# Eight of ten head blocks turned by VectorE and a trip through DRAM instead of by TensorE, in one Perceiver layer

## The chip, the core and the metric

One core of a Trainium2 chip runs the whole layer as one program. The metric is the device time of that program in microseconds (us), lower is better. Its engines work side by side, each through its own list of instructions in order: TensorE (PE; PEld is its weight load), VectorE (DVE), ScalarE (ACT), GpSimd (POOL) and SyncE (SP), which here does nothing but issue DMA transfers. An instruction waits on semaphores that other engines or landed transfers raise; while it waits, everything behind it on its engine waits too.

## The reference, cut to what matters

A layer of three parts: attention of 256 latent rows over 4096 context rows and over themselves, a Mamba block, and a mixture of 32 experts. All is 32-bit float. The change lies in the attention part:

```python
q = (x @ wq).reshape(B, L, 16, 128); k = (x @ wk).reshape(B, L, 4, 128); v = x @ wv
q = rms_norm(q, q_norm_w);  k = rms_norm(k, k_norm_w)
k_ctx = rms_norm((h_ctx_kv @ wk_ctx).reshape(B, T, 4, 128), k_norm_w);  v_ctx = h_ctx_kv @ wv_ctx
q = q * cos + rotate_half(q) * sin;  k = k * cos + rotate_half(k) * sin
scores = einsum('blhd,bmhd->bhlm', q, concat(k_ctx, k)) / sqrt(128) + mask
out = softmax(scores) @ concat(v_ctx, v);  return out @ wo
```

The scores contract over the 128 numbers of a head, so queries and keys must stand with that dimension on the partitions, while a projection leaves them with the rows on the partitions. Each block of 128 rows by 4 heads by 128 numbers must therefore be turned.

## The kernel before, in words

**Projections (5 to 84 us in the profile).** The 256 latent rows are two tiles (`t` = 0, 1). `self_block` makes one head block: four matmul steps (each is two passes in the profile) project it into `ps_self` (L211), `norm_rope` (L429 to L442) applies norm and rotation, and the returned `turn` (L464 to L469) turns it with four PE transposes into PSUM (`selfT`) and one ACT copy into `kT0` or `qT`. There are ten such blocks: two of keys (`wk`), then eight of queries (`wq[0]` to `wq[3]`, two each). Between them stand the first context tile's keys and values (`ps_k`, `ps_v`, with PE transposes `kTp`) and the latents' values (`ps_v0`). `norm_rope` goes through ACT (copy `raw`, four squares `sq` with sums `ss` in `head_squares`, L242 to L248), DVE (L437 to L440, the scale `pv` at L188) and POOL (power `r` at L189, product L441).

**Attention (from 84 us).** Stage `s` = 0 takes the latents' own keys, `s` = 1 to 8 a context tile of 512 keys each. A step is one score (`scT`, L542), its exponential on ACT (`prT`, L545), on the diagonal a mask on DVE (L548), the row sums on DVE (`lacc`, L551 or L553) and the product with the values (`oT`, L562); at the end of a pair of head group and tile DVE takes `oT` out (L566 or L568). The code keeps two steps between a score and its product. In stages 1 to 7 the keys and values of the next context tile are made beside it by a fast product (`fast_steps`): seven pieces (`p1`, `p6`, `p2`, `p7`, `p5`, `p4`, `p3`) for each half, spread evenly over the 32 steps. At the end of `p4` and `p3` a key block is normed (`key_rms`) and turned by `key_blocks` (L281 to L288): DVE transposes 32 by 32 squares, four transfers write them to DRAM tile `kd`, a fifth reads them back into `kT` as a turned block. Those transfers, the next context tile (`load_ctx`) and zeros for the experts' buffers (`clear`, L497 to L506) all go through SP's one list.

**What sets the order.** A scheduler orders every engine's list by its own estimate of when things will be ready, within the dependencies; `tc.issue_after(i)` lets what follows stand no earlier than instruction `i`, and `tc.keep_in_program_order` fixes a transfer's place among the others so marked. Tiles come from pools whose buffers are reused: `ps_tp` has one PSUM buffer (tag `tp`), `ps_mm` two, `krp` two per tag (`kraw`, `sq`), `wpool` six (`w`: `wk`, `wq[0]`, `wv`, `wq[1..3]`, then `wo[0..2]`, `fast0..2`, in that order of the code).

The fast product needs weight sums (`fast_weights`, L323 to L330: three ACT copies, and at L330 a difference on POOL that overwrites part of `wkv`) and sums of the context tile (`sums` in `fast_steps`, L342 to L345, four POOL operations per tile).

Of the kernel before, what the change touches and what calls it, by code (L numbers as in the profile page):

```python
# [11 lines left out]
FP = mybir.dt.float32  # L12
# [3 lines left out]
ALU = mybir.AluOpType  # L16
# [3 lines left out]
P = 128  # L20
L = 256
NT = L // P
DM = 512
# [4 lines left out]
NH = 16  # L28
NKV = 4
REP = NH // NKV  # L30
HD = 128
# [36 lines left out]
def perceiver_layer(ctx: ExitStack, tc: tile.TileContext, a: dict, out: bass.AP):  # L68
# [53 lines left out]
    kd = [tc.dram_tile((CK // P, NKV, HD, P), FP, name=f"kd{c}") for c in range(NC)]  # L122
    sums_d = [tc.dram_tile((SH, P), FP, name=f"sums{t}") for t in range(NT)]
# [9 lines left out]
    def layer(ctx, bounded):  # L133
# [44 lines left out]
        def wpiece(src, name):  # L178

            n = src.shape[1]  # L180
            w = wpool.tile([P, KD, 512], FP, tag="w", name=name)
            nc.sync.dma_start(w[:, :, :n], src.rearrange("(k p) n -> p k n", p=P))
            return w
# [58 lines left out]
        def head_squares(raw):  # L242

            sq = krp.tile([P, REP, HD], FP, tag="sq", name="sq")
            ss = small.tile([P, REP], FP, tag="ss", name="ss")
            for h in range(REP):
                S.activation(sq[:, h, :], raw[:, h, :], AF.Square, accum_out=ss[:, h:h + 1])  # L247
            return ss  # L248

# [12 lines left out]
        def context_tiles(c):  # L262
# [18 lines left out]
            def key_blocks(i):  # L281

                tr = krp.tile([P, NKV * HD], FP, tag="sq", name="tr")
                V.transpose(tr, raws.pop(i).rearrange("p h d -> p (h d)"))
                for b in range(0, P, 32):
                    nc.sync.dma_start(kd[c][i, :, :, b:b + 32].rearrange("h (j a) k -> a h j k", a=32),
                                      tr[b:b + 32, :].rearrange("a (h j k) -> a h j k", h=NKV, k=32))
                nc.sync.dma_start(kT[:, :, i * P:(i + 1) * P], kd[c][i].rearrange("h d k -> d h k"))  # L288
# [34 lines left out]
        def fast_weights(sums):  # L323
# [6 lines left out]
            G.tensor_tensor(b12, b22, b12, ALU.subtract)  # L330

        def fast_steps(c):
# [77 lines left out]
            sums()  # L410
# [17 lines left out]

        def norm_rope(ps, t, tb):  # L429
# [11 lines left out]
            G.tensor_tensor(o, o, r.unsqueeze(2).to_broadcast([P, REP, HD]), ALU.mult)  # L441
            return o  # L442

        kT0 = kvp.tile([P, NKV, CK], FP, tag="kT", name="kT0")
# [14 lines left out]
        def self_block(t, w, tb, dst):  # L459
            ps = ps_mm.tile([P, 512], FP, tag="mm", name="ps_self")  # L460
            project(ps, lambda k: xT[:, k, t * P:(t + 1) * P], lambda k: w[:, k, :])
            o = norm_rope(ps.rearrange("p (h d) -> p h d", d=HD), t, tb)

# [32 lines left out]

        def clear(n):  # L497

            per = -(-ROUNDS * NE // (NC - 1))
            e0, e1 = n * per, min((n + 1) * per, ROUNDS * NE)  # L500
            nc.sync.dma_start(xg[e0 * P:e1 * P, :].rearrange("(e p) d -> p e d", p=P),
                              xn[:, 0:1, :].to_broadcast([P, e1 - e0, DM]))
            if n == 0:
                for y in (ye, ye2):
                    nc.sync.dma_start(y[(NE - TAIL) * P:, :].rearrange("(e p) d -> p e d", p=P),
                                      xn[:, 0:1, :].to_broadcast([P, TAIL + 1, DM]))  # L506

        nc.sync.dma_start(by_channel, a["by_channel"])
        nc.sync.dma_start(by_head, a["by_head"].partition_broadcast(P))


        wo = [wpiece(a["wo"][j * 512:(j + 1) * 512, :], f"wo{j}") for j in range(3)]
        fast_weights(sums)
        w_x = []
# [11 lines left out]
        def bounded_attention(beside):  # L526
# [50 lines left out]
            for s in range(NC + 1):  # L577
# [6 lines left out]
                if 0 < s < NC:  # L584
                    if s + 1 < NC:
                        load_ctx(s + 1)
                    clear(s - 1)
                    extra = fast_steps(s)
# [129 lines left out]
        def mamba_memory():  # L718
# [3 lines left out]
            for t in range(NT):  # L722
                m["csT", t] = krp.tile([P, REP, HD], FP, tag="sq", name="csT")[0:SH, 0, :]
# [705 lines left out]
```

## Time and profile before

| what | us |
|---|---|
| median of 3 runs (1017.68 to 1018.71) | 1018.51 |
| the profiled execution: its time | 1019.19 |
| the profiled execution: its span | 1017.4 |
| PE busy in the span | 996.1 |
| first score of attention (`scT`) | 84.06 |
| first `ps_o` matmul (output projection) | 694.46 |

The profile is of one execution. Times in its views count from the start of the span. In a timeline line the numbers are start and duration in us, then engine, source line, operation, out<-in, shape, count, and in brackets how long the engine had been idle and who ended that. In a line of the table by stretches each engine has its busy time and, in brackets, how many instructions; then the granted TensorE clock, the share of the DMA engines, and GB/s. A PE matmul's end is modelled, and matmuls are pipelined: what counts is the distance from one start to the next. All line numbers L are those of the kernel before unless "after" is said.

### The profile page before, as it was taken

What the parts mean: (1) busy time and instruction counts of PE and PEld (TensorE: products, weight loads), DVE (VectorE), ACT (ScalarE), POOL (GpSimd) and SP (SyncE); (2) the same over time, 40 slices, a digit from 0 to 9 for tenths busy, and PEclk for the clock granted to TensorE, in tenths of its full rate; (3) what the DMA queues carried; (4) which work ended last, traced back from release to release, by engine and by line L of the source; (5) the groups of instructions that cost most, each with busy time, mean ns of one, the idle gap of its engine ahead of it and who ended that gap; (6) DMA issues with size and microseconds to landing.
All of it is one profiled execution on the core that took longest, in us unless ns stands there. A gap on an engine that the chain in (4) does not pass through costs nothing.

```text
span 1017.4 us, 9099 instructions
## 1 busy us (share of the span) xinstructions
PE 996.1 (98%) x2818; PEld 480.9 (47%) x2818; DVE 495.4 (49%) x975; ACT 384.6 (38%) x870; POOL 156.9 (15%) x156
## 2 busy tenths in 40 slices
PE   7999999999999999999999999999999999999997
PEld 3444444444444444444444444444656554555553
DVE  4347454445444454544544544575885653322233
ACT  3456444443443443443443434442445431222210
POOL 4343001001001101100200200000131322000022
PEclk9999999999999999999999999999999999999999
DMA  9997021110210301301301202500264358999833
GB/s 335 375 404 303 0 42 50 34 31 30 64 26 16 83 11 32 82 10 32 83 2 40 63 0 42 156 10 0 94 200 148 114 208 318 357 353 371 291 116 95
DMA packets 115435, 127.73 MB, mean 126 GB/s; under 512 B 63377, under 2 KB 78642, under 8 KB 114226
## 3 DMA queue, kind: packets, MB, share of 16 engines
q1 hardware_dynamic: 108272, 111.52, 33.9%
q0 software_dynamic: 2208, 8.39, 2.3%
q10 hardware_dynamic: 4898, 7.16, 1.9%
q8 instruction: 24, 0.39, 0.2%
q14 instruction: 33, 0.27, 0.1%
HBM read 88.76 MB, written 38.29 MB: 125 GB/s over the span
## 4 chain that ended last, share of the span: by engine, by line
PE 91%; DMA 2%; DVE 2%; POOL 2%; issue 1%; ACT 1%; SPq 0%; POOLq 0%; DVEq 0%; ACTq 0%
PE oT L562 23%; PE scT L542 22%; PE ps_kv L350 17%; PE ps_egu L211 7%; PE ps_self L211 3%; PE ps_ye L1256 2%; PE ps_o L754 2%; PE ps_ye L1259 1%; PE ps_v L211 1%; PE ps_k L211 1%; PE ps_xbc L211 1%; PE ps_out L944 1%; PE xgTp L1201 1%; PE total L1247 1%; DMA lm<-sums 1%
## 5 line engine op out<-in xcount | busy, mean ns | idle before, releaser
L553 DVE TENSOR_TENSOR lacc<-lacc,prT 128x512 f32<-128x512 f32 x260 | 182.7, 704 | 246.3 <-ACT prT L545 245.5
L545 ACT ACTIVATE prT<-scT,bq,rk 128x512 f32<-128x512 f32 x256 | 198.3, 775 | 228.0 <-PE scT L542 223.1
L562 PE MATMUL oT<-prT,v 128*128 128x512 f32 x536 | 272.2, 592 | 1.3 <-DVE prT L548 1.3
L542 PE MATMUL scT<-qT,kT 128*128 128x512 f32 x536 | 272.3, 592 | 0.0
L562 PEld LDWEIGHTS oT<-prT,v 128*128 128x128 f32 x536 | 101.7, 190 | 129.4 <-issue 109.3
L542 PEld LDWEIGHTS scT<-qT,kT 128*128 128x128 f32 x536 | 101.2, 190 | 124.6 <-issue 123.1
L189 POOL TENSOR_TENSOR rk<-pv,mhalf 128x4 f32<-128x4 f32 x32 | 32.3, 1011 | 357.8 <-DVE pv L188 357.1
L247 ACT ACTIVATE sq<-kraw 128x128 f32<-128x128 f32 x128 | 38.3, 301 | 94.0 <-DVE kraw L368 93.9
L1216 DVE TENSOR_TENSOR hid<-si,ps_egu 128x128 f32<-128x128 f32 x32 | 9.2, 288 | 94.2 <-ACT si L1214 94.2
L350 PE MATMUL ps_kv<-fast,fast 128*128 128x512 f32 x112 | 52.6, 592 | 0.0
L350 PE MATMUL ps_kv<-wkv,fast 128*128 128x512 f32 x112 | 52.6, 592 | 0.0
L350 PE MATMUL ps_kv<-wkv,ctx 128*128 128x512 f32 x112 | 52.6, 592 | 0.0
L568 DVE TENSOR_TENSOR oacc<-oT,oacc 128x512 f32<-128x512 f32 x64 | 43.7, 683 | 0.0
L1170 POOL DMA_INDIRECT yk<-ye,row_y x12 | 13.3, 1105 | 137.5 <-PE ps_egu L211 134.1
L350 PEld LDWEIGHTS ps_kv<-wkv,ctx 128*128 128x128 f32 x112 | 21.3, 190 | 26.8 <-issue 23.7
L350 PEld LDWEIGHTS ps_kv<-fast,fast 128*128 128x128 f32 x112 | 21.3, 190 | 26.8 <-issue 21.8
L350 PEld LDWEIGHTS ps_kv<-wkv,fast 128*128 128x128 f32 x112 | 21.3, 190 | 26.8 <-issue 23.4
L1262 ACT COPY y_sb<-ps_ye 128x512 f32<-128x512 f32 x26 | 15.2, 586 | 48.8 <-PE ps_ye L1259 43.0
L368 DVE TENSOR_TENSOR kraw<-ps_kv,fast 128x256 f32<-128x256 f32 x42 | 17.9, 425 | 31.6 <-PE ps_kv L350 31.6
L1214 ACT ACTIVATE si<-ps_egu 128x192 f32<-128x192 f32 x32 | 10.6, 332 | 58.5 <-PE ps_egu L211 58.5
L754 PE MATMUL ps_o<-wo,qT 128*128 128x512 f32 x64 | 28.8, 592 | 0.0
L211 PE MATMUL ps_self<-wq,xT 128*128 128x512 f32 x64 | 28.6, 592 | 0.0
(294 smaller groups left out, 1129.6 us busy)
## 6 DMA issues: line engine op xcount, KB each, us to landing
xg<-xn SPq DMA_DIRECT2D x6, 2560.0 KB, 21.5
w_in<-in_pairs_dram SPq DMA_DIRECT2D x14, 768.0 KB, 6.9
ctx<-in_ctxT_dram SPq DMA_DIRECT2D x7, 1024.0 KB, 5.0
kd<-tr SPq DMA_DIRECT2D x112, 64.0 KB, 2.4
kT<-kd SPq DMA_DIRECT2D x28, 256.0 KB, 2.8
xg_sb<-xg SPq DMA_DIRECT2D x28, 256.0 KB, 6.3
ye<-y_sb ACTq DMA_DIRECT2D x26, 256.0 KB, 7.1
wkv<-in_pairs_dram SPq DMA_DIRECT2D x6, 768.0 KB, 6.8
```

The costliest lines, as they stand in the source:

```text
L189: return G.tensor_tensor(dst, v[:, :n], mhalf[:, :n], ALU.pow)
L211: TE.matmul(ps, lhs(k), rhs_of(k), start=(k == 0), stop=(k == KD - 1))
L247: S.activation(sq[:, h, :], raw[:, h, :], AF.Square, accum_out=ss[:, h:h + 1])
L350: TE.matmul(ps, lhs(k), rhs(k), start=(start and k == 0), stop=(k == 1), skip_group_check=True)
L368: V.tensor_tensor(to[n], ps[:, n, :], more[:, n, :], ALU.add)
L542: TE.matmul(sc, kT[:, g, i * P:(i + 1) * P], qT[:, t, heads4(g), :].rearrange("p h q -> p (h q)"), start=True, stop=True)
L545: S.activation(pr, sc, AF.Exp, bias=shift, scale=SCALE if r is None else r[:, i, g:g + 1])
L553: V.tensor_tensor(la, la, pr, ALU.add)
L562: TE.matmul(outs[g, t], v[:, i, g * HD:(g + 1) * HD], pr, start=(n == 0), stop=last)
L568: V.tensor_tensor(ov, outs.pop((g, t)), ov, ALU.add)
L754: TE.matmul(m["ps_o", t], aT[:, t, h, :], wo[j][:, h % 4, :], start=(h == 0), stop=(h == NH - 1))
L1256: TE.matmul(ps[i], h[:, i, :], wd[:, i, :], start=True, stop=False)
```

## The change

1. A helper `turn_heads(dst, src, by)` is made of what `key_blocks` did. `self_block` calls it, with a new DRAM tile `qd`, for the two key blocks and the query blocks of `wq[0]`, `wq[1]`, `wq[2]`: eight blocks. The two of `wq[3]` stay on PE.
2. In the helper the four writes and the read are kept in program order, so that on SP's list each read stands directly behind its own four writes. The DVE tile `tr` gets a tag of its own (two buffers).
3. `head_squares` puts its squares, which nobody reads, into the PSUM buffer `tp` instead of the SBUF tag `sq`.
4. The zeros (`clear`) of each stage are no longer issued at the stage's start but as an extra piece in the middle of `fast_steps`'s list, kept in program order; before, nothing kept them from being issued early. The list has 15 entries instead of 14, and so its pieces fall on other steps.
5. `fast_weights` stands before the `wo` loads, so it takes the buffers of `wk`, `wq[0]`, `wv`; the `wo` loads, `by_channel` and `by_head` are kept in program order behind the turned blocks' transfers.
6. POOL's difference for the fast weights (L330) may stand no earlier than the last head block's product; the first tile's `sums` no earlier than the fifth block's.

```diff
-        def wpiece(src, name):
+        def wpiece(src, name, order=lambda dma: dma):
...
-            nc.sync.dma_start(w[:, :, :n], src.rearrange("(k p) n -> p k n", p=P))
+            order(nc.sync.dma_start(w[:, :, :n], src.rearrange("(k p) n -> p k n", p=P)))
...
         def head_squares(raw):
-            sq = krp.tile([P, REP, HD], FP, tag="sq", name="sq")
+            sq = ps_tp.tile([P, REP, HD], FP, tag="tp", name="sq")
...
+        def turn_heads(dst, src, by):
+            tr = krp.tile([P, REP * HD], FP, tag="tr", name="tr")
+            V.transpose(tr, src.rearrange("p h d -> p (h d)"))
+            pin = tc.keep_in_program_order
+            for b in range(0, P, 32):
+                pin(nc.sync.dma_start(by[:, :, b:b + 32].rearrange("h (j a) k -> a h j k", a=32),
+                                      tr[b:b + 32, :].rearrange("a (h j k) -> a h j k", h=REP, k=32)))
+            pin(nc.sync.dma_start(dst, by.rearrange("h d k -> d h k")))
...
             def key_blocks(i):
-                tr = krp.tile([P, NKV * HD], FP, tag="sq", name="tr")
-                V.transpose(tr, raws.pop(i).rearrange("p h d -> p (h d)"))
-                for b in range(0, P, 32):
-                    nc.sync.dma_start(kd[c][i, :, :, b:b + 32].rearrange("h (j a) k -> a h j k", a=32),
-                                      tr[b:b + 32, :].rearrange("a (h j k) -> a h j k", h=NKV, k=32))
-                nc.sync.dma_start(kT[:, :, i * P:(i + 1) * P], kd[c][i].rearrange("h d k -> d h k"))
+                turn_heads(kT[:, :, i * P:(i + 1) * P], raws.pop(i), kd[c][i])
...
-            G.tensor_tensor(b12, b22, b12, ALU.subtract)
+            with tc.issue_after(heads_done[-1]):
+                G.tensor_tensor(b12, b22, b12, ALU.subtract)
...
-            sums()
+            with tc.issue_after(behind) if behind else nullcontext():
+                sums()
...
-            G.tensor_tensor(o, o, r.unsqueeze(2).to_broadcast([P, REP, HD]), ALU.mult)
+            heads_done.append(G.tensor_tensor(o, o, r.unsqueeze(2).to_broadcast([P, REP, HD]), ALU.mult).ins)
...
             o = norm_rope(ps.rearrange("p (h d) -> p h d", d=HD), t, tb)
+            if bounded and w is not wq[3]:
+                return turn_heads(dst, o, qd.pop())
...
+        zeros = lambda to, z: tc.keep_in_program_order(nc.sync.dma_start(to, z))
...
-        nc.sync.dma_start(by_channel, a["by_channel"])
-        nc.sync.dma_start(by_head, a["by_head"].partition_broadcast(P))
-        wo = [wpiece(a["wo"][j * 512:(j + 1) * 512, :], f"wo{j}") for j in range(3)]
+        pin = tc.keep_in_program_order
+        pin(nc.sync.dma_start(by_channel, a["by_channel"]))
+        pin(nc.sync.dma_start(by_head, a["by_head"].partition_broadcast(P)))
         fast_weights(sums)
+        wo = [wpiece(a["wo"][j * 512:(j + 1) * 512, :], f"wo{j}", pin) for j in range(3)]
...
-                    clear(s - 1)
-                    extra = fast_steps(s)
+                    extra = fast_steps(s, heads_done[4] if s == 1 else None)
+                    extra.insert(len(extra) // 2, lambda: clear(s - 1))
```

The order that the scheduler makes of it, in the built program: the eight groups of PE transposes are gone, and on SP's list eight groups of four writes and a read stand between the last weight and context loads and `by_channel`. At the start of attention PE's list was `scT` x3, `oT`, `selfT`, then `scT` and `oT` by turns; after the change it is:

```
selfT x4, scT x3, oT, selfT x4, scT, oT, scT, oT, scT, oT x3,
ps_kv x2 (p1), ps_kv x2 (p6), scT, oT, scT x3, oT, scT, oT, ...
```

At the start of stage 8 the list before was `scT`, `oT` x3, `scT` x3, `oT`; after, it is `scT`, `oT` x3, `scT`, `oT`, `scT` x3, `oT`.

More of the change, by code (lines that the diff above doesn't have):

```diff
@@ L1 @@
-from contextlib import ExitStack
+from contextlib import ExitStack, nullcontext
 import numpy as np
@@ L122, in perceiver_layer @@
     kd = [tc.dram_tile((CK // P, NKV, HD, P), FP, name=f"kd{c}") for c in range(NC)]
+    blocks_d = [tc.dram_tile((REP, HD, P), FP, name=f"qd{i}") for i in range(NT * NH // REP)]
     sums_d = [tc.dram_tile((SH, P), FP, name=f"sums{t}") for t in range(NT)]
@@ L329, in fast_weights, with fast_steps @@
                 S.copy(fast[n], t)
-            G.tensor_tensor(b12, b22, b12, ALU.subtract)
-        def fast_steps(c):
+            with tc.issue_after(heads_done[-1]):
+                G.tensor_tensor(b12, b22, b12, ALU.subtract)
+        def fast_steps(c, behind=None):
             ct = ctx_tiles.pop(c)
@@ L427, in rope_table @@
                 V.scalar_tensor_tensor(tb[:, 1, :, half(i)], rope[:, :, 1, :], 2.0 * i - 1.0, wb[1 - i], ALU.mult, ALU.mult)
+        heads_done = []
         def norm_rope(ps, t, tb):
@@ L440, in norm_rope @@
             V.tensor_tensor(o, o, u, ALU.add)
-            G.tensor_tensor(o, o, r.unsqueeze(2).to_broadcast([P, REP, HD]), ALU.mult)
+            heads_done.append(G.tensor_tensor(o, o, r.unsqueeze(2).to_broadcast([P, REP, HD]), ALU.mult).ins)
             return o
+        qd = list(blocks_d)
         kT0 = kvp.tile([P, NKV, CK], FP, tag="kT", name="kT0")
@@ L500, in clear @@
             e0, e1 = n * per, min((n + 1) * per, ROUNDS * NE)
-            nc.sync.dma_start(xg[e0 * P:e1 * P, :].rearrange("(e p) d -> p e d", p=P),
-                              xn[:, 0:1, :].to_broadcast([P, e1 - e0, DM]))
+            zeros(xg[e0 * P:e1 * P, :].rearrange("(e p) d -> p e d", p=P),
+                  xn[:, 0:1, :].to_broadcast([P, e1 - e0, DM]))
             if n == 0:
                 for y in (ye, ye2):
-                    nc.sync.dma_start(y[(NE - TAIL) * P:, :].rearrange("(e p) d -> p e d", p=P),
-                                      xn[:, 0:1, :].to_broadcast([P, TAIL + 1, DM]))
-        nc.sync.dma_start(by_channel, a["by_channel"])
-        nc.sync.dma_start(by_head, a["by_head"].partition_broadcast(P))
-        wo = [wpiece(a["wo"][j * 512:(j + 1) * 512, :], f"wo{j}") for j in range(3)]
+                    zeros(y[(NE - TAIL) * P:, :].rearrange("(e p) d -> p e d", p=P),
+                          xn[:, 0:1, :].to_broadcast([P, TAIL + 1, DM]))
+        pin = tc.keep_in_program_order
+        pin(nc.sync.dma_start(by_channel, a["by_channel"]))
+        pin(nc.sync.dma_start(by_head, a["by_head"].partition_broadcast(P)))
         fast_weights(sums)
+        wo = [wpiece(a["wo"][j * 512:(j + 1) * 512, :], f"wo{j}", pin) for j in range(3)]
         w_x = []
@@ L722, in mamba_memory @@
             for t in range(NT):
-                m["csT", t] = krp.tile([P, REP, HD], FP, tag="sq", name="csT")[0:SH, 0, :]
+                m["csT", t] = krp.tile([P, REP, HD], FP, tag="tr", name="csT")[0:SH, 0, :]
             off = [krp.tile([P, REP, HD], FP, tag="kn", name="off") for _ in range(2)]
```

## The prediction

> **What bounds the kernel.** I read the totals first, then the clock, then busy time by stretches. TensorE is busy nearly all the time at full clock.
>
> ```profile
> PE 996.1 (98%) x2818; PEld 480.9 (47%) x2818; DVE 495.4 (49%) x975; ACT 384.6 (38%) x870; POOL 156.9 (15%) x156
> ...
> PEclk9999999999999999999999999999999999999999
> ```
>
> The stretches are the projections, the start of attention, the rest of stage 0 and stages 1 to 8.
>
> ```profile
> 24.00:84.00 60.00, 59.71 (x175) 28.59 (x175) 26.30 (x49) 30.76 (x119) 28.82 (x26) 1.00 1.03 392
> 84.00:92.00 8.00, 6.39 (x20) 2.76 (x18) 7.62 (x10) 5.46 (x10) 5.30 (x4) 1.00 1.05 409
> 92.00:109.00 17.00, 17.00 (x41) 7.49 (x40) 12.44 (x22) 10.32 (x16) 0.00 (x0) 1.00 0.20 76
> 109.00:688.00 579.00, 579.00 (x1351) 256.37 (x1350) 284.82 (x470) 234.89 (x506) 58.75 (x52) 1.00 0.18 41
> ```
>
> So a microsecond of PE work taken out is worth a microsecond, as long as PE is not made to wait; idle PE exists in one place that the change touches, 84 to 92 us, where DVE is full (7.62 of 8.00). The DMA engines are full until then (share 1.03), but PE waits for none of it: the waits of PE there are these two.
>
> ```profile
> PE oT L562 <- DVE prT L548: 1.3, 1, 1.3
> PE selfT L467 <- POOL lacc L441: 0.6, 2, 0.3
> ```
>
> PE's own timeline shows what a turned block costs and where the idle stands.
>
> ```profile
> 71.94 0.60 PE L467 MATMUL selfT<-ident,lacc 128*128 128x128 f32 x4
> 72.38 3.60 PE L211 MATMUL ps_self<-wq,xT 128*128 128x512 f32 x8
> 76.26 0.66 PE L467 MATMUL selfT<-ident,lacc 128*128 128x128 f32 x4 [0.29 <-POOL lacc L441]
> ...
> 84.06 2.74 PE L542 MATMUL scT<-qT,kT 128*128 128x512 f32 x6
> 88.08 1.12 PE L562 MATMUL oT<-prT,v 128*128 128x512 f32 x2 [1.28 <-DVE prT L548]
> 89.54 0.66 PE L467 MATMUL selfT<-ident,lacc 128*128 128x128 f32 x4 [0.33 <-POOL lacc L441]
> 90.03 1.02 PE L542 MATMUL scT<-qT,kT 128*128 128x512 f32 x2
> ```
>
> Last, two pairs of rows from the timelines of POOL, DVE and ACT.
>
> ```profile
> 84.27 2.53 POOL L330 TENSOR_TENSOR wkv<-wkv 128x1024 f32<-128x1024 f32 x1
> ...
> 84.52 2.31 DVE L188 TENSOR_SCALAR pv<-ss 128x4 f32<-128x4 f32 x1
> ...
> 91.09 0.69 ACT L545 ACTIVATE prT<-scT,bq 128x512 f32<-128x512 f32 x1 [0.28 <-PE scT L542]
> ...
> 91.81 0.69 DVE L548 TENSOR_TENSOR prT<-prT,upper 128x512 f32<-128x512 f32 x1 [0.25 <-ACT prT L545]
> ```
>
> The first pair: a DVE operation on SBUF that starts beside a POOL operation ends only when that has ended (a 0.15 us scale took 2.31). The second pair is the latency of a diagonal step: score at 90.03, exponential 1.06 later, mask 0.72 after that, 0.69 long.
>
> **The sum.** It is made in the profiled execution (span 1017.4, time 1019.19, 1.8 outside the span); the median is 0.7 below that execution, and I carry the difference over to the median 1018.51.
>
> *Removed from PE.* Four transposes take 0.44 (71.94 to 72.38) or 0.43: eight blocks, 8 x 0.43 = 3.44. One of them (76.26) also waited: from the start of the last projection's second half to it there are 0.45 too many; that goes. So the first score, at 84.06, comes at about 80.2. The eight ACT copies that go (0.59 each) are beside PE and worth nothing.
>
> *The old idle at the start of attention.* Three scores end at 84.06 + 3 x 0.86 = 86.64, the product starts at 88.08: 1.44. The last turn loses 0.49 by start times. These 1.93 belong to an order of lists that no longer exists; I take them out and put in what the new lists give.
>
> *New idle 1, DVE behind POOL.* Before, POOL did the last two context sums (L344, L345) and the difference L330 between 81 and 87, ahead of the last head's power. After, the difference must follow the last head's product, and those two sums come behind it: all three stand where the first masks run. Net of waiting they last 2.3, 1.2 and 1.2 (2.53, 1.74 and 1.46 in the rows, with DVE operations inside), 4.7 together. DVE's list there is mask, row sum, the transpose of the last `wq[2]` block, mask, row sum, `oT` copy, row sum, mask. Stepping both lists by such durations, the row sum waits for the difference, the second mask for one sum, the next row sum for the other; PE idles 0.3, 0.7 and 1.7 before the first three products and 0.5 more for a PSUM buffer that DVE has not emptied: 3.2. The same stepping gives the old lists 3.0 for the measured 0.45 + 1.93 = 2.4, so I take 3.2 x 2.4 / 3.0 = 2.6. Ends: 0 (92 to 109 us, where no POOL work runs, PE has no idle) and 4.7 (all of it on PE).
>
> *New idle 2 and 3, a score directly before its own product.* PE's new list has this once in stage 0: 1.06 + 0.72 + 0.69 + 0.05 - 0.86 = 1.66. Once more at the start of stage 8, without a mask (exponential there 0.78 by the table): 1.06 + 0.78 + 0.05 - 0.86 = 1.03. Both are chains of measured latencies, with nothing on PE between; I give them 0.2 either way.
>
> *Added beside PE, at nothing.* Eight DVE transposes of 0.70 (28 such rows at 701 to 712 ns): DVE is busy 26.3 of 60. DVE does wait in its list for POOL's power and product (1.0 + 1.0) before a transpose, some 5.1 per block with the rotation (2.05), scale and transpose; a pair of blocks with the value projection between pairs comes every 10.3. Without that cover PE would wait for a free projection bank: the second rival. Eight times five transfers on SP: four issues of 0.5, landing 2.4, issue 0.4, landing 2.8, about 7.4 per block, the read blocking SP until the writes have landed. Behind it stand only the next blocks' transfers, `by_channel`, `by_head` and `wo` (needed at 694). The last block's transpose is at about 86, its landing at 93.5, its first score, behind `p1` and `p6`, at about 100.5: 7 in hand. In stages 1 to 7 a read now goes before the next block's writes, no later than before; PE has 579.00 of 579.00 there, so nothing is won and the old slack stays. The zeros: 2560 KB are 6.7 at the 392 GB/s of the full queue, in stage 1 with two of 1792 KB 16; the next transfers on the list come some 30 later. If that cover were gone, key blocks would be late by the rest. The 15th entry shifts pieces by at most one step (1.7 to 2.6): nothing, bounded by 0.5 in each of seven stages.
>
> *Squares into PSUM.* No row shows ACT writing PSUM. A square takes 0.30, its accumulator read 0.19, and the distance is 0.30; each square now waits for the one before it, so up to 0.41, 0.4 more per block, against ACT's idle of about 0.9 before every exponential. I take nothing; ends: 0 and 0.1 per key block, 2.8. [...]
>
> Sum: -3.44 - 0.45 - 1.93 + 2.6 + 1.66 + 1.03 = -0.5. **Forecast 1018.0**, no change that a measurement can tell (0.2%, 2.0 us, is about what it can).
>
> The rule that speaks against the change: a turned block costs DVE 0.70 and five transfers where PE needs 0.43. [...]
>
> **Rivals.**
>
> *The pile-up does not come* (POOL's three operations fall between DVE's): new idle 1 is 0, 1018.0 - 2.6 = 1015.4. For: order between two engines that exclude each other hangs on tenths. Against: three POOL operations of 4.7 cannot miss a DVE that is full there. Halved, it gives 1016.7, still inside 0.2%. Chance 0.14.
>
> *The projections become DVE's* (this is also the change not doing what it says: PE waits where it transposed). Place: 24 to 80. Point: when a block takes DVE over 5.15 on average, so that `raw` and then the projection banks fill. Price: at most the 3.44 won, 1021.4. For: 5.1 is close, and POOL contention stretches single DVE rows to 1.5. Against: for part of the blocks the next rotation fills the wait for POOL, and the first six blocks have two extra projections between them. Chance 0.07.
>
> *ACT late in stages 1 to 7*, by the squares' waits. Point: an exponential that ends over two steps, 3.4, behind its score. Price 28 x 0.1 = 2.8, so 1020.8. Against: the idle 0.9 per step. Chance 0.07.
>
> **How the numbers follow.** The forecast's case has 0.72, spread over 1016.5 to 1020.0 by new idle 1 (-2.6 to +2.1) and the smaller bounds. Faster by over 0.2%: 0.14, the first rival; slower: 0.14, the other two. With a tenth left out on either side the range is 1015.8 to 1020.6.
>
> **What would show it.** First score at 80.2 (right if 79.7 to 80.7; the second rival if later, with PE gaps before `ps_self`). PE idle between it and the first product of stage 1's pieces some 4.3 in place of 1.93, with the DVE rows beside the three POOL operations stretched; one gap of 1.0 near 662; none elsewhere up to the first `ps_o` at 694.0. A PE wait for `kT` or `qT` transfers, or an exponential row behind squares with PE idle after it, would prove the covers wrong.

## The result, and the profile after

The changed kernel takes 1020.67 us (median of 16 runs, 1017.16 to 1023.75); the kernel before, in as many runs beside it, 1018.07 (1017.24 to 1019.08). The ratio is 1.0025, with a 95% interval of 1.0015 to 1.0034: slower by 2.6 us, where 1018.0 was forecast and a change in either direction within 0.2%. The profiled execution of the changed kernel took 1020.27 us with a span of 1018.5, so it is a usual one. From here on, "before" and "changed" are these two kernels.

First the page of the changed kernel: TensorE's busy time fell by 1.5 us, not by 3.4, and its clock row ends in an 8 where before it had a 9.

```profile
PE 994.6 (98%) x2786; PEld 477.5 (47%) x2786; DVE 502.3 (49%) x983; ACT 392.0 (38%) x862; POOL 155.8 (15%) x156
...
PEclk9999999999999999999999999999999999999998
```

The table by stretches of the changed kernel answers to the one of before (24 us, first score, 92, 109, 688): the idle of TensorE lies where the prediction put it, 1.66 us in the second row, 1.55 in the third, 0.92 in the fourth, none in the first.

```profile
24.00:79.70 55.70, 55.70 (x143) 25.20 (x141) 29.83 (x58) 30.80 (x110) 25.41 (x24) 1.00 0.51 140
79.70:92.00 12.30, 10.64 (x28) 4.20 (x27) 10.45 (x13) 7.76 (x13) 7.90 (x5) 1.00 0.29 65
92.00:109.00 17.00, 15.45 (x37) 6.61 (x36) 9.78 (x18) 7.60 (x12) 0.00 (x0) 1.00 0.54 188
109.00:688.00 579.00, 578.08 (x1348) 255.69 (x1347) 287.92 (x471) 242.08 (x505) 58.56 (x52) 1.00 0.27 77
```

TensorE's timeline in the changed kernel, at the start of attention and of stage 8. The first score starts at 79.70; the waits in brackets are the three "new idles".

```profile
79.70 2.74 PE L559 MATMUL scT<-qT,kT 128*128 128x512 f32 x6
...
89.85 1.12 PE L579 MATMUL oT<-prT,v 128*128 128x512 f32 x2 [1.22 <-DVE prT L565]
91.34 1.96 PE L579 MATMUL oT<-prT,v 128*128 128x512 f32 x4 [0.36 <-DVE oacc L583]
...
99.14 1.12 PE L579 MATMUL oT<-prT,v 128*128 128x512 f32 x2 [1.55 <-DVE prT L565]
...
663.39 1.12 PE L579 MATMUL oT<-prT,v 128*128 128x512 f32 x2 [0.92 <-ACT prT L562]
```

So attention did what was forecast. To see where the time came from, cut both executions at five starts on TensorE: the ninth pass of the first key projection (`ps_k`), the first `ps_o` (694.30 us before, by the timeline; 694.46, in the table further up, is where the chain of waits takes it up), the last `ps_out`, the first `hid_sp` (the first of the last three expert pairs), and the last `total`.

| us | start to `ps_k` | to `ps_o` | to last `ps_out` | to `hid_sp` | tail, to last `total` |
|---|---|---|---|---|---|
| before | 11.65 | 682.64 | 127.74 | 156.07 | 32.98 |
| changed | 11.14 | 682.40 | 126.50 | 156.06 | 36.17 |
| difference | -0.51 | -0.24 | -1.24 | -0.01 | +3.19 |

The first column is when the first loads land and has nothing to do with the change (in all profiles without extra work at the start it lies between 11.1 and 11.9, and two profiles of the changed kernel itself have 11.14 and 11.88). Attention gained 0.24. Two stretches that the diff does not touch moved by far more, in opposite directions.

**The tail.** TensorE's `total` of the last pair but one waits for `hidS`, a copy on VectorE; the copy stands behind VectorE's additions of gathered rows (`x_sb<-yk`), those wait for POOL's gathers (`yk<-ye`), and the first gather waits for the last store to `ye`. Rows of ACT, POOL and PE from the timelines, before:

```profile
979.86 0.33 ACTq L1264 DMA_DIRECT2D ye<-y_sb  x1
...
982.88 0.99 POOL L1170 DMA_INDIRECT yk<-ye,row_y  x1 [134.13 <-PE ps_egu L211]
...
1001.02 3.70 PE L1247 MATMUL total<-kT,hidS 128*128 128x512 f32 x8 [1.13 <-DVE hidS L1240]
```

and changed, with the row of VectorE that keeps `hidS` back:

```profile
977.86 0.33 ACTq L1281 DMA_DIRECT2D ye<-y_sb  x1
...
982.48 0.99 POOL L1187 DMA_INDIRECT yk<-ye,row_y  x1 [135.75 <-DVE hid L1234]
...
998.93 0.75 DVE L1194 SCALAR_TENSOR_TENSOR x_sb<-yk,lacc,x_sb 128x512 f32<-128x512 f32 x1 [0.57 <-DMA yk<-ye,row_y]
999.60 0.85 DVE L1257 COPY hidS<-rest_sp 64x256 f32<-64x256 f32 x2
...
1000.50 5.40 PE L1264 MATMUL total<-kT,hidS 128*128 128x512 f32 x8 [2.62 <-DVE hidS L1257]
```

The store is issued 2.0 us earlier, but the first gather starts 4.62 behind it instead of 3.02. In the trace the 16 shares of the store land 1.83 to 2.02 us after the issue before; in the changed kernel 14 of them by 2.03, one at 2.25 and the last at 3.33. What else ran is in the changed kernel's DMA view for 977 to 981 us (queue, kind: packets, MB, share of the 16 engines):

```profile
q8 instruction: 1, 0.02, 1.8%
q14 instruction: 1, 0.01, 0.6%
```

A fetch of instructions: 16 KB on queue 8 from 978.46 to 979.60, and 8 KB at 979.45. In the kernel before, the same view for 979 to 983 us has only the store's queue; its fetch on queue 8 came at 971.13.

The eight matmuls behind the wait then took 5.40 us instead of 3.70. The table by stretches (last but two: the granted clock) says why: the clock is at half for 3.41 us.

```profile
998.00:1001.92 3.92, 1.42 (x4) 0.70 (x5) 2.72 (x6) 0.00 (x0) 1.13 (x1) 1.00 0.48 145
1001.92:1005.33 3.41, 3.41 (x6) 1.35 (x5) 1.39 (x5) 0.00 (x0) 0.00 (x0) 0.50 0.01 2
```

So the tail's 3.19 are 1.5 of longer wait (2.62 - 1.13), from a gather that comes 1.6 later, and 1.7 of half clock.

**The middle.** Here it is the kernel before that was hit. `sums` goes to DRAM (ACT's queue) and comes back as `lm` (POOL's queue); `ps_out` waits at the end of what follows. Before, then changed, from the timelines:

```profile
777.44 0.33 ACTq L810 DMA_DIRECT2D sums<-csT  x1
...
780.24 0.65 POOL L811 DMA_DIRECT2D lm<-sums  x1 [3.39 <-PE ps_xbc L211]
...
796.07 7.13 PE L944 MATMUL ps_out<-w_out,qT 128*128 128x512 f32 x16 [1.86 <-DVE qT L938]
```

```profile
776.68 0.33 ACTq L827 DMA_DIRECT2D sums<-csT  x1
...
778.58 0.65 POOL L828 DMA_DIRECT2D lm<-sums  x1 [2.49 <-PE ps_xbc L212]
...
794.08 7.13 PE L961 MATMUL ps_out<-w_out,qT 128*128 128x512 f32 x16 [0.75 <-DVE qT L955]
```

2.80 us from the store to the read before, 1.90 after; TensorE's wait ahead of `ps_out` is 1.86 before, 0.75 after. A 16 KB fetch on queue 8 started at 777.4 before, in the same tenth of a microsecond as the store; in the changed kernel it started at 778.3, 1.6 us behind the store.

**Theory 1**: queue 8 carries TensorE's instructions. The change takes 32 transposes with 32 weight loads off TensorE (2818 to 2786 matmuls in the page), 64 instructions, so every later fetch comes at another point of the program; one moved off the `sums` store (a gain) and one onto the last `ye` store (a loss), and TensorE's longer wait there let the clock fall. **Theory 2**: the loss comes from something else in the change (its transfers, its zeros, its order), at other places in each execution, as the spread of 6.6 us might suggest.

### The profile page after: what moved, and what is told of

It is laid out like the page before. It is cut to its first block, busy times and chain, and to the rows that moved or that the text cites. A ratio compares the mean times of both kernels' runs of the same rounds, so it can differ in the third digit from the quotient of the medians.

```text
span 1018.5 us, 9069 instructions
## 1 busy us (share of the span) xinstructions
PE 994.6 (98%) x2786; PEld 477.5 (47%) x2786; DVE 502.3 (49%) x983; ACT 392.0 (38%) x862; POOL 155.8 (15%) x156
## 4 chain that ended last, share of the span: by engine, by line
PE 91%; DVE 2%; issue 2%; POOL 1%; DMA 1%; ACT 1%; SPq 0%; DVEq 0%; POOLq 0%; ACTq 0%
PE oT L579 22%; PE scT L559 22%; PE ps_kv L356 16%; PE ps_egu L212 8%; PE ps_self L212 3%; PE ps_ye L1273 2%; PE ps_v L212 2%; PE ps_o L771 2%; PE ps_xbc L212 1%; PE ps_ye L1276 1%; PE ps_k L212 1%; PE ps_out L961 1%; PE xgTp L1218 1%; PE total L1264 1%; PE ps_yd L901 1%
## 5 line engine op out<-in xcount | busy, mean ns | idle before, releaser
L570 DVE TENSOR_TENSOR lacc<-lacc,prT 128x512 f32<-128x512 f32 x260 | 185.4, 714 | 240.7 <-ACT prT L562 239.8
L248 ACT ACTIVATE sq<-kraw 128x128 f32<-128x128 f32 x128 | 35.6, 278 | 44.9 <-DVE kraw L374 42.8
```

The lines of the kernel that those rows point to most:

```text
L570: V.tensor_tensor(la, la, pr, ALU.add)
```

## The experiments

All kernels in one table, with the same cuts; what was added to each is told below. "Gather" is from the issue of the last `ye` store to the first gather, "fetch" where TensorE's 16 KB fetch nearest to the first `hid_sp` starts (us from it). Times are medians of 5 to 16 runs (2 for the one with its zeros back); the stretches are of one profile each. The ratio is to the kernel before on the same chip; not all rows ran on the same one, so two rows are best compared by their ratios.

| kernel | median | ratio, 95% | to `ps_o` | to `ps_out` | fetch | gather | tail |
|---|---|---|---|---|---|---|---|
| before | 1018.07 | 1 | 682.64 | 127.74 | -7.0 | 3.02 | 32.98 |
| changed | 1020.67 | 1.0015-1.0034 | 682.40 | 126.50 | +2.4 | 4.63 | 36.17 |
| changed, run again | 1020.60 | 1.0005-1.0023 | 682.30 | 126.50 | +2.3 | 4.79 | 36.10 |
| before, copies on ACT | 1016.98 | 0.9977-0.9995 | 682.75 | 126.77 | -6.9 | 3.03 | 31.61 |
| changed, copies on ACT | 1018.11 | 0.9993-1.0012 | 682.40 | 126.72 | +2.4 | 4.65 | 33.18 |
| changed, wait filled | 1019.66 | 1.0006-1.0024 | 682.41 | 126.49 | +2.4 | 4.74 | 35.01 |
| changed, 24 heavy | 1025.57 | 1.0056-1.0083 | 682.31 | 126.51 | -12.9 | 3.34 | 32.89 |
| changed, 12 light | 1018.54 | 0.9997-1.0015 | 682.41 | 127.48 | -6.9 | 3.46 | 33.02 |
| before, 12 light | 1017.58 | 0.9990-1.0008 | 682.64 | 126.50 | -12.5 | 3.03 | 32.66 |
| changed, 12 light, copies | 1017.31 | 0.9985-1.0003 | 682.41 | 127.25 | -6.9 | 3.35 | 31.96 |
| changed, 12 light, zeros back | 1031.32 | 1.0111-1.0148 | 695.47 | 127.15 | -6.4 | 3.01 | 32.63 |
| before, 45 light | 1018.68 | 0.9996-1.0014 | 682.68 | 126.50 | +4.8 | 3.04 | 32.74 |
| before, 48 light | 1019.62 | 1.0000-1.0018 | 682.75 | 126.50 | +2.4 | 4.13 | 33.72 |
| changed, 24 light | 1017.75 | 0.9986-1.0004 | 682.41 | 126.51 | -12.9 | 3.34 | 33.20 |
| before, 12 light, copies | 1016.63 | 0.9977-0.9995 | 682.65 | 126.50 | -12.6 | 3.02 | 31.58 |
| changed, 24 light, copies | 1016.77 | 0.9975-0.9993 | 682.41 | 126.50 | -12.5 | 3.35 | 31.96 |
| the same, loop's order | 1014.69 | 0.9951-0.9978 | 678.92 | 128.09 | -12.5 | 3.33 | 32.04 |
| the same, run again | 1014.93 | 0.9950-0.9977 | 679.30 | 128.10 | -12.5 | 3.34 | 31.91 |
| before, 12 light, copies, loop's order | 1019.25 | 0.9999-1.0019 | 683.89 | 128.21 | -12.5 | 3.04 | 31.68 |

The stretch from the last `ps_out` to the first `hid_sp` is left out of the table: it is 156.05 to 156.07 in every one.

### Taking TensorE out of the gathers' chain

Two copies of the last pair but one go from VectorE to ScalarE (ACT):

```diff
-                    V.tensor_copy(hs[half, 2, :], rest[half, i, :])
+                    (S.copy if n == NP - 2 else V.tensor_copy)(hs[half, 2, :], rest[half, i, :])
```

In the changed kernel:

> The changed kernel, with the two copies hidS<-rest_sp of the last pair but one made by ScalarE instead of VectorE, so that TensorE's last wait no longer stands behind VectorE's additions of the gathered rows. Theory 1 (the change's gain of 2.0 us reaches the experts, and is lost in the tail, where TensorE waits for the additions of gathered rows and the granted clock then falls to half): the wait of 2.6 us ahead of total<-kT,hidS is gone, the clock stays at full, the time falls by 2.6 + 1.7 to about 1016.4 us, 1.7 below before, and its spread shrinks to that of before (about 2 us). Theory 2 (the time is lost at other places, another one in each execution): the wait goes, but the time falls by no more than before's own wait of 1.1 us, to about 1019.5, and the spread of over 5 us stays.

In the kernel before:

> The kernel before with the same two copies on ScalarE. Both theories: its wait of 1.1 us ahead of total<-kT,hidS goes, the time falls by 1.0 to 1.2, to about 1017.0 us. Theory 1 then has the changed kernel with these copies about 0.6 to 2.0 us faster than this one (its lead of 2.0 at the experts, less nothing); theory 2 has it 2 us slower.

The kernel before did as expected: 1016.98, the tail 31.61, its wait gone. The changed kernel lost the half clock and 2.6 us, but not all of it: 1018.11, between the 1016.4 of theory 1 and the 1019.5 of theory 2, so the time decides nothing. In the trace the gather is as late as ever (4.65), and VectorE's late additions now stand ahead of the last pair's `hid` instead. TensorE's timeline in the changed kernel with the copies on ACT:

```profile
996.63 5.31 PE L1264 MATMUL total<-kT,hidS 128*128 128x512 f32 x12
1003.27 1.13 PE L1250 MATMUL hid_sp<-xc,hid 128*128 128x256 f32 x4 [1.33 <-DVE hid L1233]
```

The gathers' chain is what sets the end, and it is later by 1.6 to 1.8 us in all four profiles of the changed kernel with its fetch at this place (4.63 to 4.79 against 3.02). That speaks for one fixed cause, against theory 2, by which the loss would be at another place in each execution.

### Moving TensorE's instruction count

Matmuls that nobody reads, at TensorE's start, where it waits for the first loads; each of them is four instructions (two passes, each with its weight load). First 24 heavy ones:

```diff
+        if bounded:
+            early_ps = ps_tp.tile([P, REP, HD], FP, tag="tp", name="early_ps")
+            for _ in range(24):
+                TE.matmul(early_ps[:, 0, 0:8], ident, ident[:, 0:8], start=True, stop=True)
```

> The changed kernel, with 24 matmuls of 8 columns put at TensorE's start, where it waits for the first loads; they do nothing but move the instruction count of TensorE by 48. Theory 1 with the code fetch (in the changed kernel a fetch of 16 KB for TensorE at 978.46 us shares a DMA engine with the last store to ye, issued at 977.86, one sixteenth of which lands at 981.18 instead of 979.9, and the first gather waits for it): the fetch comes 4 to 7 us earlier, the last store lands within 2.1 us of its issue, the first gather starts 3.0 us after that issue as in before instead of 4.6, TensorE's wait ahead of total<-kT,hidS is about 1.1 to 1.3 us, the clock stays full, the time falls to about 1017.5 us. If the fetch does not hold the store: the first gather stays 4.6 us behind the issue and the time at 1020.7.

They took 10.4 us and put the whole program back by some 7.9 us (the ninth `ps_k` pass at 19.12), so the time, 1025.57 for an expected 1017.5, says nothing by itself. They are also 96 instructions and not the 48 that the expectation counted. The tail does tell: the fetch moved to 12.9 us ahead of `hid_sp`, the gather to 3.34, the wait to 1.04, the clock stayed full, and the tail took 32.89. Then 12 light ones (16 by 8 columns, 0.79 us for all, inside the wait), in the changed kernel and as a control in the kernel before:

```diff
+            for _ in range(12):
+                TE.matmul(early_ps[0:16, 0, 0:8], ident[:, 0:16], ident[:, 0:8], start=True, stop=True)
```

> The changed kernel, with 12 matmuls of 16 by 8 columns at TensorE's start, light enough to end within the wait for the first loads; they only move TensorE's instruction count by 48. Theory 1 with the code fetch: the 16 KB fetch for TensorE, which starts 2.4 us behind the first hid_sp in three runs of the changed kernel and its variants, starts 2 to 4 us ahead of it; the first gather starts 3.0 us behind the last store to ye instead of 4.6, TensorE's wait ahead of total<-kT,hidS is 1.1 to 1.3 us, the clock stays full, and the time is about 1017.5 us (1017.0 to 1018.1), which is the 0.5 of the prediction below before. If the fetch was not the cause: 1020.7 and the first gather still 4.6 us behind.

> The kernel before with the same 12 light matmuls at the start: a control for what they cost themselves. Its fetch starts 7.0 us ahead of the first hid_sp and moves to about 13 us ahead, where no store to ye is under way that a gather waits for. Both theories: no change, 1018.1 us (1017.8 to 1018.5).

The tail went as expected (33.02), and the time fell by 2.1 us; but not to 1017.5, because 48 instructions put the changed kernel's fetches where before has its own, onto the `sums` store: 127.48 in the middle instead of 126.50. The control's fetch left that store (126.50); its median is 0.3 to 0.5 us lower, which its interval does not tell from nothing (0.9990 to 1.0008). Both kernels have now been seen with and without that hit. In the five profiles whose fetch starts within about 0.1 us of the store the read comes 2.52 to 2.95 us behind it, in all the others 1.89 or 1.90; the stretch takes 126.77 to 127.74 with it and 126.49 to 126.72 without (the loop's order apart), so it costs 0.3 to 1.2 us, not in step with the read; what makes the difference was not traced. With the copies as well:

> The changed kernel with the 12 light matmuls and with the two copies hidS<-rest_sp of the last pair but one on ScalarE. Theory 1: no wait of TensorE in the tail; the stretch from the first hid_sp to the last total takes 31.6 us as in the kernel before with these copies (33.2 in the changed kernel with the copies alone), and the time is that kernel's 1017.0 less the 0.5 that the change saves: about 1016.5 us (1016.0 to 1016.9), the fastest of all. If the fetch was not the cause: 1018.1 as without the 12 matmuls.

1017.31: the tail is free of waits (31.96), the middle is hit (127.25). So 24 light ones, which put the fetches where the control has them, clear of both stores, without and with the copies, and the kernel before with 12 and the copies:

> The changed kernel with 24 of the light matmuls, 96 instructions, so that its code fetches lie as those of the kernel before with 12 do, which meet neither sums<-csT (fetch 76.9 us behind the first ps_o) nor the last store to ye (13 us ahead of the first hid_sp). Theory 1: the stall ahead of ps_out is 0.9 us (1.9 with 12 of them), the stretch from the first hid_sp to the last total 32.7 to 33.0, and the time is that of the kernel before with 12 of them, 1017.6, less the 0.25 to 0.5 us that the change saves up to the first ps_o: about 1017.2 us (1016.8 to 1017.6). If code fetches explain only part: 1018.0 or more.

> The kernel before with 12 light matmuls and with the two copies hidS<-rest_sp of the last pair but one on ScalarE. Theory 1: no stall in the tail (31.6 us from the first hid_sp to the last total) and 0.9 us ahead of ps_out instead of 1.2: 1017.0 less 0.3, about 1016.7 us.

> The changed kernel with 24 light matmuls and with the two copies on ScalarE: the same places of the code fetches as in the run before this one. Theory 1: 0.25 to 0.5 us less than the kernel before with the copies and 12 light matmuls, about 1016.3 us (1015.9 to 1016.7). If it is no faster than that kernel, the change saves nothing at all once both are free of the fetches.

With TensorE's fetches out of the way the changed kernel takes 1017.75 and the kernel before 1017.58 (ratios to before 0.9995 and 0.9999, both intervals with 1 in them); with the copies, side by side, 1016.77 and 1016.63. By the last expectation's own measure the change then saves nothing. It gains 0.24 up to `ps_o` and loses 0.4 to 0.5 in the tail, where the gather is still 0.3 later than in before's kernels (3.34 against 3.03) though the store lands as early (2.04 us after its issue). Fetches of 8 KB on queue 14 lie beside it in these kernels (at 979.8 and 981.4 us with the gather at 981.5, in the changed kernel with 24 light matmuls) and in none of before's. One more run fits: the changed kernel with its zeros back (below) has no such fetch between store and gather, and its gather is at 3.01 as in before's. Whose code that is, and whether it is the cause, was not tried.

### Putting the fetch onto the store in a kernel without the change

How far apart the fetches lie in the instruction list is an estimate from the trace: in the kernel before 255 TensorE rows lie between neighbouring fetches on average, 198 to 321 singly. If it were 255 each time, 48 light matmuls, 192 instructions, would give the kernel before about the same places of the fetches as the 64 fewer of the changed kernel (32 transposes with their weight loads), and 45, 180 instructions, those of 75 fewer. The kernel before with 45 of them, and nothing of the change:

> [...] Theory 1 (the code fetch): the fetch starts about 2.4 us behind the first hid_sp instead of 7 ahead, the last store to ye lands late, the first gather starts 4.4 to 4.8 us behind its issue instead of 3.0, and the stretch from the first hid_sp to the last total takes 34.5 us, or 36.2 where the clock also falls to half, instead of 33.0; in exchange lm<-sums, 0.6 to 1.0 us late with a fetch at 83.1 us behind the first ps_o, is issued on time at 85.0. Time 1018.9 to 1021.0 us, with 0 to 1 us of it from the 45 matmuls themselves. If the tail's loss comes from something else in the change (its transfers, its zeros, its order): the tail stays at 33.0 and the time at 1018.0 to 1019.0.

The fetch came 4.8 us behind `hid_sp`, past the store, and not the 2.4 that were expected; the tail stayed at 32.74. The `sums` part was right (126.50). With 48:

> [...] With 45 the fetch came 4.8 us behind the first hid_sp, past the last store, and the tail kept 32.7 us. Theory 1: with 48 it comes 2.4 us behind, as in the three traces of the changed kernel at that count; the first gather starts 4.4 to 4.8 us behind the last store's issue (3.0 with 45), TensorE waits 2.4 to 2.8 us ahead of total<-kT,hidS, and the tail takes 34.5 us (36.2 if the clock falls to half); the time is 1.5 to 3 us over the 1018.7 of 45: 1020.2 to 1021.7 us. If the tail's loss is not the fetch's: 1018.7 and a tail of 32.7 to 33.0 us.

With three more matmuls the fetch starts at +2.4 as in the changed kernel. The DMA view of that stretch, and the rows of ACT, POOL and PE:

```profile
q8 instruction: 1, 0.02, 1.7%
```

```profile
979.44 0.33 ACTq L1268 DMA_DIRECT2D ye<-y_sb  x1
...
983.57 0.98 POOL L1174 DMA_INDIRECT yk<-ye,row_y  x1 [135.25 <-DVE hid L1221]
...
1001.35 3.70 PE L1251 MATMUL total<-kT,hidS 128*128 128x512 f32 x8 [1.88 <-DVE hidS L1244]
```

15 shares of the store land by 2.02 us after the issue, the last at 3.13; the gather starts at 4.13; the wait is 1.88 where 45 matmuls had 0.9; the tail is 33.72, one microsecond longer. The median, 1019.62, is under the expected 1020.2 to 1021.7; it is 0.9 above that with 45, but on another chip, and by the ratios (1.0009 and 1.0005) half of that, within the noise. So the time does not show the hit here; the trace does, in the late share, the late gather and the longer wait, in a kernel that has nothing of the change and with no other fetch beside the store. The gather's delay was expected at 1.6 and is 1.1: the rest of the changed kernel's 1.6 is 0.2 by which its last share landed later (3.33), and the 0.3 above that stays open. With a wait of 1.88 the clock did not fall.

### The clock

Four matmuls of 128x512 on a spare bank, in TensorE's wait:

```diff
+                if n == NP - 2:
+                    spare = self.ps_x.tile([P, DM], FP, tag="x", name="spare")
+                    for _ in range(4):
+                        TE.matmul(spare, h[:, 0, 0:P], wd[:, 0, :], start=True, stop=True)
```

> The changed kernel, with four matmuls of 128x512 on a spare bank put ahead of the last pair but one's total<-kT,hidS, 1.9 us of work inside TensorE's wait of 2.6 us. Theory 1: the wait itself stays where it ends, TensorE's idle time there is 0.7 to 0.9, the clock no longer falls to half, and the time falls by 1.7 to about 1019.0 us. If the clock falls for another reason: it falls all the same, and the time stays at about 1020.7, or is longer by up to 1.9.

```profile
996.26 3.60 PE L1265 MATMUL spare<-kT,hidS 128*128 128x512 f32 x8
999.69 5.31 PE L1268 MATMUL total<-kT,hidS 128*128 128x512 f32 x12
```

The clock stayed full in the profile. The four matmuls took 3.4 us, not 1.9 (0.86 each, not 0.47), and so ended 0.8 after the wait would have; 1.7 less 0.8 is 0.9, and the median fell by 1.0, to 1019.66. The single runs say the same as the two profiles: their mean granted clock is 0.999 or 1.000 in all 11 here, and 0.998 or less in 14 of the 16 of the changed kernel.

The changed kernel once more, with nothing added:

> The changed kernel itself, a second look. Theory 1: the same tail as in its first profile, the last store's landing shared with the fetch 2.4 us behind the first hid_sp, the first gather 4.4 to 4.8 us behind the store's issue, TensorE idle for 2.4 to 2.8 us ahead of total<-kT,hidS; whether the clock falls to half behind it may differ from one execution to the next, by 1.7 us, and the median is 1019.5 to 1021.0. If the first profile showed a chance event, the first gather starts 3.0 us behind the store's issue and the median is near 1018.

Everything came again: the fetch, the gather 4.79 behind the store, a wait of 2.73, and 3.41 us at half clock. The late store is therefore no chance event. What remains of the spread (1017.47 to 1021.96 here) is not settled; the mean clock of single runs differs (0.997 to 1.000), so the fall need not be there in every one of them.

### The zeros

```diff
-        zeros = lambda to, z: tc.keep_in_program_order(nc.sync.dma_start(to, z))
+        zeros = lambda to, z: nc.sync.dma_start(to, z)
...
+                    clear(s - 1)
                     extra = fast_steps(s, heads_done[4] if s == 1 else None)
-                    extra.insert(len(extra) // 2, lambda: clear(s - 1))
```

> The changed kernel with the 12 light matmuls, and with its zeros back at the start of each stage and not kept in program order, so that they may be put among the turned heads' stores and reads. The prediction held that the zeros cost nothing where they now stand. If they also cost nothing here, the time is that of the kernel with the 12 matmuls. Expected: the zeros of 2.6 MB each (13.9 to 21.8 us from issue to landing in the kernel before) come between each block's stores and its read; each of the 8 reads comes 6 to 15 us later, the first score waits, and the time is 1035 to 1075 us.

1031.32, some 4 us under the expected 1035 to 1075. The scheduler put one zero transfer between each block's stores and its read. The waits of TensorE between 60 and 130 us now name what the prediction had costed at nothing, the turned blocks' reads (7.2 us beside 4.7 for VectorE's masks), and the clock fell to half twice, for 6.8 us each:

```profile
PE scT L563 <- DMA qT<-qd: 7.2, 3, 4.3
```

```profile
95.80:102.60 6.80, 3.43 (x4) 1.46 (x5) 1.94 (x4) 0.69 (x1) 0.00 (x0) 0.50 1.10 324
...
109.40:116.20 6.80, 5.17 (x6) 2.02 (x7) 2.08 (x4) 1.98 (x3) 0.00 (x0) 0.50 0.77 241
```

So fixing the zeros' place is no detail of the change: it is worth 12.8 us (1031.32 against 1018.54), and without it the turned heads lose: 1.0111 to 1.0148 times the kernel before.

### The order

The score and value matmuls of the first and last stage held in the loop's order (`pin` is the kernel's own name for it), with 24 light matmuls and the copies on ACT:

```diff
+                keep = pin if s in (0, NC) else (lambda mm: mm)
-                TE.matmul(sc, kT[:, g, i * P:(i + 1) * P], ...)
+                keep(TE.matmul(sc, kT[:, g, i * P:(i + 1) * P], ...))
...
-                TE.matmul(outs[g, t], v[:, i, g * HD:(g + 1) * HD], pr, start=(n == 0), stop=last)
+                keep(TE.matmul(outs[g, t], v[:, i, g * HD:(g + 1) * HD], pr, start=(n == 0), stop=last))
```

> The changed kernel with 24 light matmuls and the two copies on ScalarE, and with the score and value matmuls of the first and the last stage of attention held in the order in which the loop writes them, so that no score stands directly ahead of its own product there (the prediction's second and third new idle time, 1.72 us at 99.1 and 1.08 at 663.4 us). If these idle times are the order's alone, both go, and the time falls from 1016.8 by up to 2.8 us to 1014.0 to 1014.6 us. If something else is late there (the additions on VectorE that free the banks), they come back elsewhere, and the time is 1016 to 1017 us.

1014.69. Then its counterpart, the kernel before in the same order, and the changed one again beside it:

> The kernel before with 12 light matmuls, the two copies on ScalarE, and the score and value matmuls of the first and the last stage held in the loop's order: what the ordering alone is worth without the change. Its order was already the loop's in these stages, with no stall like those of the changed kernel at 99.1 and 663.4 us. Theory 1 (the stalls belong to the changed kernel's order): no change against the same kernel without the ordering, 1016.6 us (1016.2 to 1016.9), so the whole of the change then saves 1.9 us against it. If the ordering is worth as much here: about 1014.6.

> The changed kernel in the loop's order again, beside the one above on the same chip: 1014.7 us (1014.2 to 1015.2), 1.9 us less than the kernel before in the same dress, because the 32 transposes (3.4 us) are off TensorE and the two new stalls (2.8 us) are gone, less the stall at the first products.

1014.93 for the changed kernel (ratio to before 0.9950 to 0.9977), 3.2 us under before; the two are the fastest seen. Both stalls are gone and 3.1 to 3.5 us with them (to `ps_o` 679.30 and 678.92); 1.6 come back in the middle (128.09). There pinning stage 8 also moves the pieces of the next part that are woven into it: TensorE waits 0.90 ahead of `ps_dt` at 716.74, where it did not wait without the order, and 0.28 ahead of `ps_csT` at 729.98; the rest was not traced. For the kernel before I had expected the ordering to be neutral, but it costs 2.6: 1.2 up to `ps_o` (a wait of 0.9 for a key block's read shows at 666) and 1.7 in the middle. Against the best version of the kernel before (1016.63), which is not in this order, the change with the order saves 1.7 to 1.9 us.

## Why the prediction was wrong, by its own steps

*Removed from PE, 3.44 and 0.45.* Right: the first score came at 79.70; without the earlier start (0.51) that is 80.21, and 80.2 was forecast.

*New idles.* Right in place and nearly in size: by start times 2.3 for the gaps behind POOL's pile-up (2.6 forecast), 1.72 (1.66) and 1.08 (1.03). The pile-up came as described: the first row sum, a copy on VectorE (L568 after) that takes 0.43 at 99 us, took 2.46 at 82.45, beside POOL's difference of 2.80. But not every VectorE operation is held so, as the prediction has it: the transpose at 84.83 took its usual 0.70 inside POOL's sum of 84.58 to 86.04.

*Sum up to `ps_o`.* -0.5 was forecast, -0.24 is measured. The gaps were 0.2 smaller than taken, but the matmuls behind the gaps took about 0.1 longer, from their start to the next (0.97 from 99.14 to 100.11, against 0.86), which the sum left out, and there are six such matmuls after the change against two before.

*Beside PE, at nothing.* Right: no wait of TensorE for `qT` or `kT`, none before `ps_self`, none in stages 1 to 7. The squares into PSUM, bounded by 2.8, came out 0.02 us shorter each (on average 278 ns against 301 for the keys') and cost nothing. A turned block took 7.0 to 7.5 us from its transpose to the landing of its read, in the four whose landing the trace has; the prediction's 7.4, whose terms add up to 7.6, was near. The cover of the zeros is real and is the move itself, as its removal shows.

*The step that failed* is the first one: "So a microsecond of PE work taken out is worth a microsecond, as long as PE is not made to wait; idle PE exists in one place that the change touches". I let everything behind the first `ps_o` follow it unchanged. Two things in it were wrong. First, the end of this program hangs on chains of transfers, at 780 to 796 and at 980 to 1001 us, and both waits stood in the profile of before (the tail's 1.13 in TensorE's timeline, `lm<-sums` with 8.61 us in the chain of waits); I did not read these stretches, since the diff does not name them. Second, the transposes were costed as 0.43 us each block and not as 64 entries in TensorE's instruction list. Taking them out moved the fetches of that list, one off a store (from 777.4 to 778.3 us), one onto a store (from 971.13 to 978.46). The measured terms that the sum lacked: -0.3 to -1.2 in the middle, +1.6 for the gathers, +1.7 for the clock. They make -0.24 - 0.3 + 1.6 + 1.7 = 2.8 with the smaller value of the middle, and the medians differ by 2.6; with the larger, which the two profiles have, it is 1.8. That the smaller one is usual in the kernel before is an assumption.

*The carry from the profiled execution to the median* was wrong as well: the profiled execution of before was 1.1 above the median of its 16 runs. The hit in the middle may be 1.0 of that (127.74, where the kernel before with copies at nearly the same fetch had 126.77); one profile cannot show it.

*The rivals.* None of the three happened. Two of them ended at 1021.4 and 1020.8, near the measured time, but neither of their mechanisms is in the trace. The spread named for the forecast's own case does not follow from its terms: 1018.0 with -2.6 to +2.1 is 1015.4 to 1020.1, not 1016.5 to 1020.0.

*The clock.* In the tail of the changed kernel the clock was at half for 3.41 us, in the kernel with its zeros back twice for 6.8 us. The tail's waits of TensorE of up to 1.88 us did not bring it, those of 2.62 and 2.73 did; what decides it between these was not shown.

*The fetches.* The page of the kernel before has 24 of them on queue 8, of 16 KB each:

```profile
q8 instruction: 24, 0.39, 0.2%
```

Eleven of them start between 109 and 688 us, where TensorE was busy for 579.00 of 579.00 us: they cost TensorE nothing there. The transfers beside two of them did pay: in the changed kernel the store to `ye` has its last share 3.33 us after its issue instead of 2.02, in the kernel before the read of `sums` comes 2.80 us behind the store instead of 1.90.

## What to carry to other kernels

Before you let a gain run through to the end, read the last wait of every later stage, whether the diff touches it or not; if a stage ends on a chain of transfers, a gain on the busy engine only makes that engine wait longer, and the wait can cost clock as well (here waits of 2.62 and 2.73 us did, 3.41 us at half clock each). When an edit adds or removes instructions on an engine, a difference of 1 or 2 us far behind the edit may be where its code fetches fall (here 0.3 to 1.2 us in the middle and 1.6 at the gathers): put a few idle instructions at the start of both kernels and compare them at several counts before you credit or blame the edit. Compare stretches between fixed instructions, not ends: here the 156 us between the last `ps_out` and the first `hid_sp` agreed to 0.02 us in all kernels, so that half a microsecond elsewhere could be placed.

## What the runs showed of the hardware that I had not expected

In the changed kernel, and in the kernel before with 48 light matmuls, a 16 KB code fetch starts 0.6 us after the issue of the 256 KB store to `ye`. The last of the store's 16 shares then landed 3.33 us after the issue in the changed kernel and 3.13 in the other, instead of 2.02, and the first gather, which waits for the whole store, started 4.63 and 4.13 us behind the issue instead of 3.02 (4.79 in the changed kernel run again); with 45 light matmuls, whose fetch starts 2.4 us later, it started at 3.04. Whether the fetch and the late share were on one DMA engine was not shown. Where such a fetch started within about 0.1 us of the 8 KB store at 777 us, that store's reader started 2.52 to 2.95 us behind it, against 1.89 or 1.90 elsewhere. The fetches did not move evenly with the instruction count: 48 instructions more moved the one in the tail by 9.3 us in the changed kernel (+2.4 to -6.9) and by 5.6 in the kernel before (-7.0 to -12.5), and 12 instructions decided whether it met the store (+4.8 or +2.4). The clock stayed full behind a wait of TensorE of 1.88 us in the tail and was at half for 3.41 us behind one of 2.62.
